# A graph and expert kernel on one core: the first expert slot's first layer, tile by tile

## The chip, the cores and the metric

The kernel runs on one core of a Trainium2 chip. The metric is the device time of one execution in microseconds; lower is better. A core has a matrix engine (PE, with its weight loads shown as PEld), a vector engine (DVE), a scalar engine (ACT), a general engine (POOL) and a queue engine (SP) that here only issues DMAs. Each engine works through its own queue in order. Matmul results go to PSUM, an on-chip memory that PE writes and that DVE and ACT read; everything else is kept in SBUF. Engines are held in step by semaphores: an instruction waits until those that it depends on have ended.

## What is computed

The reference takes 2048 tokens of 256 features and 67584 weighted edges, and does two steps:

```python
x = x + gnn(layernorm(x))      # out[dst] += w * x[src], plus a bias per node
x = x + ffn(layernorm(x))      # 8 experts, the best 2 of a token, mixed by their shares

# ffn, for the experts that a token is sent to:
xe = xn * ln_g + ln_b
h  = gelu(xe @ W1 + b1)        # 256 -> 1024
y  = h @ W2 + b2               # 1024 -> 256
out += share * y
```

The change lies in the second step, in the first expert slot that is worked on.

## The kernel before

**The first half** (to about 230 us) turns the edge list into dense 128x128 blocks and multiplies them with the normalized tokens; dense() (line 375) does the last of these matmuls, and add (line 386) adds them into acc on DVE.

**Routing and slots.** The 2048 tokens are routed in two batches: first_b, the first 10 blocks of 128 tokens, and last_b, the other 6. For each batch DVE takes the two best experts of each token and gives every choice a place in its expert's list. The experts then work in *slots*: a slot is 256 rows (TT = 2 tiles of P = 128) of one expert. Three slots (EARLY = 3) begin before the second batch is routed: whole[0], whole[1] and whole[2], filled from first_b alone. Later slots are loaded by load_slot (line 989), and some at the end hold one tile only (128 rows, "half slots").

**What one slot does.** Each step is a function:
- get_rows (line 978): POOL issues one indirect DMA per tile that gathers the rows of the slot into xs. In the first slots the features come from x1_d, the shares from sh_d.
- turn_rows (line 1006): PE transposes xs, two 128x128 blocks per tile (KD = 2), into the PSUM tile px, after some "warm" matmuls of the identity. scale_rows (line 1023): two DVE instructions of 128x256 scale and shift px into xeT, one for each k.
- layer_1 (line 1044): for each of 8 chunks c (KH = 8), PE multiplies two k-blocks of W1 with xeT into a new PSUM tile ph of 128x256 (a pool of 3 such tiles, ps_h), and ACT applies Gelu with a bias and writes hT[:, c]. A matmul on f32 data shows as two instructions, so a chunk is 4 instructions and a layer 32. A dictionary "between" says what else is to be emitted before a given chunk.
- set_weights (line 1031) prepares each row's share, and layer_2 (line 1059) multiplies hT with W2, tile by tile, scales on DVE (line 1070) and sends the rows out by an indirect DMA (line 1075).

**What sets the order.** From line 697 on the code stands under tc.manual_schedule for all engines but POOL: each of PE, DVE, ACT and SP works through its instructions in the order in which the code emits them. Which instruction waits for which is worked out by the framework from the tiles that they read and write.

**The stage of the change** (lines 1154 to 1195). In order of the code: the last add of the first half; the shares of first_b; POOL's gathers for the three early slots; then

```python
roots(last_b)                      # ACT
turn_rows(whole[0], 6)             # PE: 6 warm matmuls, 4 transposes; DVE: 2 scales
enlist_rows(first_b)               # DVE, f16, 128x2560
count(first_b); take_seen(last_b)  # DVE
...                                # put_acc on SP; scales, logits, best, select of last_b on DVE
hT = layer_1(whole[0], {4: list_batch_0, 7: lambda: sum_counts(last_b)})
```

list_batch_0 (line 1168) emits list_rows(first_b), 20 matmuls of the two lists that enlist_rows and enlist_low made, and an ACT copy of the result. sum_counts (line 779) is PE's counting of last_b and needs sel, the end of DVE's chain of small instructions. After layer_1 come ACT's scale_recs and two table loads, DVE's places and lists of last_b, PE's transposes for whole[1] (head, line 1019), and layer_2 of whole[0].

Of the kernel before, what the change touches and what calls it, by code (L numbers as in the profile page):

```python
# [10 lines left out]
F32 = mybir.dt.float32  # L11
# [3 lines left out]
AF = mybir.ActivationFunctionType  # L15
OP = mybir.AluOpType
# [6 lines left out]
P = 128  # L23
# [4 lines left out]
def kernel(  # L28
# [30 lines left out]
    nc = tc.nc  # L59
# [5 lines left out]
    KD = D // P  # L65
    KH = H // P
# [13 lines left out]
    TS = 256  # L80
# [71 lines left out]
    ident = consts.tile([P, P], F32, name="ident")  # L152
# [239 lines left out]
    with tc.manual_schedule(engines=ALL):  # L392
# [99 lines left out]
        for n in range(NH):  # L492
# [32 lines left out]
            g, k = divmod(n - NB // 2, NB // 2)  # L525
            if g >= 0:
                late.append(dense(GROUPS[g], 2 * k))
            if n == 0:
# [9 lines left out]
                for k in range(KD):  # L538
                    nc.tensor.matmul(tr[:, nt:nt + NE], ones, wr_sb[:, k, :], start=(k == 0),
                                     stop=(k == KD - 1))  # L540
# [4 lines left out]
                for lo, m in ((0, KH), (KH, KD), (KH + KD, KD)):  # L545
# [9 lines left out]
                    op0=OP.mult, op1=OP.add)  # L555
# [42 lines left out]
    with tc.If(n_used < E):  # L598
# [4 lines left out]
        for b in range(NB):  # L603
            nc.vector.tensor_scalar(acc[:, b, :D], acc[:, b, :D], nv_c[:, b:b + 1], None,
                                    op0=OP.add)
# [9 lines left out]
        with tc.tile_pool(name="any", bufs=2) as anyp, tc.tile_pool(  # L615
            name="ps_any", bufs=2, space=PSUM
# [4 lines left out]
            with tc.For_i(0, E // P, 1) as t:  # L621
# [18 lines left out]
                for b in range(NB):  # L640
                    hot = anyp.tile([P, P], F32, name="hot")
                    nc.vector.tensor_scalar(hot, iota_p, s_b[:, b:b + 1], w_t, op0=OP.is_equal,
                                            op1=OP.mult)
# [9 lines left out]
    slotp = right("slot", 2)  # L653
    ps_x = ctx.enter_context(tc.tile_pool(name="ps_x", bufs=1, side="right", space=PSUM))
# [6 lines left out]
    def new_set(pool, i, n=TT):  # L661
        return (
            pool.tile([P, n, RW], F32, name=f"xs{i}"),
            pool.tile([P, KD, H], F32, name=f"w1_{i}"),
            pool.tile([P, KH, D], F32, name=f"w2_{i}"),
            pool.tile([P, KH + 2 * KD], F32, name=f"ec{i}"),
            pool.tile([P, D], F32, name=f"b2_{i}"),
        )
# [14 lines left out]
    sets = [new_set(wpool, i) for i in range(AHEAD + 1)]  # L683
    tos = [wpool.tile([P, TT], I32, name=f"to_i{i}") for i in range(AHEAD + 8)]
    heads = [new_head(wpool, i) for i in range(2)]

    LAST = SURE - EARLY - 2
    whole = []
    for i in range(EARLY + NF):
        k = i - EARLY if i - EARLY < LAST else i - EARLY + 2  # L690
# [6 lines left out]
    with tc.manual_schedule(engines=ALL - {ET.Pool}):  # L697
# [10 lines left out]
        def batch(i, b, n):  # L708
            return {"i": i, "b": b, "n": n, "full": [P, n, NE]}
# [62 lines left out]
        def count(s):  # L772

            sel = s["sel"]
            more = route.tile([P, NE], F32, name=f"more{s['i']}", bufs=1)
            nc.vector.tensor_reduce(more, sel.rearrange("p b e -> p e b"), AX.X, OP.add)
            nc.vector.tensor_add(seen, seen, more)

        def sum_counts(s):

            sel, seen_b = s["sel"], s["seen"]
            s["pc"] = pc = counts[:, s["i"], :s["n"], :]
            nc.tensor.matmul(pc, before, sel, start=True, stop=False)
            nc.tensor.matmul(pc, ones_b, seen_b[:, None, :].to_broadcast(s["full"]), start=False,
                             stop=False)
            for d in range(1, s["n"]):
                nc.tensor.matmul(pc[:, d:, :], ones_b, sel[:, :s["n"] - d, :], start=False,
                                 stop=(d == s["n"] - 1))
            s["all"] = counts[:, 2 + s["i"], 0, :]
            nc.tensor.matmul(s["all"], ones_b, seen_b, start=True, stop=False)  # L790
            for j in range(s["n"]):
                nc.tensor.matmul(s["all"], ones_b, sel[:, j, :], start=False,
                                 stop=(j == s["n"] - 1))
# [74 lines left out]
        def enlist_rows(s):  # L868
            n, in_hi = s["n"] * 2, s["in"][1]
            hot = [P, n, P // 2, 2]  # L870
            tk = tok1[:, s["b"]:s["b"] + s["n"], :].rearrange("p b (i t) -> p (b i) t", t=2)
            nc.vector.tensor_tensor(split(in_hi), split(in_hi), tk[:, :, None, :].to_broadcast(hot),
                                    OP.mult)
# [132 lines left out]
        def turn_rows(s, warm=0):  # L1006


            xs = sets[s.set][0]
            pt = ps_x.tile([P, KD, TS], F32, name="px")  # L1010
            for i in range(warm):
                nc.tensor.matmul(pt[:, 0, :P], ident, ident, start=True, stop=True)
            for t in range(s.n):
                for k in range(KD):
                    nc.tensor.transpose(pt[:, k, t * P:(t + 1) * P],  # L1015
                                        xs[:, t, k * P:(k + 1) * P], ident)
            scale_rows(s, pt)
# [26 lines left out]
        def layer_1(s, between={}):  # L1044
            xs, w1, w2, ec, b2r = sets[s.set]
            xeT = heads[s.head][0]
            hT = slotp.tile([P, KH, TS], F32, name="hT")
            for c in range(KH):
                if c in between:
                    between[c]()  # L1050
                ph = ps_h.tile([P, TS], F32, name="ph")[:, :s.n * P]
                for k in range(KD):
                    nc.tensor.matmul(ph, w1[:, k, c * P:(c + 1) * P], xeT[:, k, :],  # L1053
                                     start=(k == 0), stop=(k == KD - 1))
                nc.scalar.activation(hT[:, c, :s.n * P], ph, AF.Gelu, bias=ec[:, c:c + 1],  # L1055
                                     scale=1.0)
            return hT

        def layer_2(s, hT, put, between={}):
            w2 = sets[s.set][2]  # L1060
            xeT, wt, b2w = heads[s.head]
            for t in range(s.n):
                if t in between:
                    between[t]()
                py = ps_y.tile([P, D], F32, name="py")
                for c in range(KH):
                    nc.tensor.matmul(py, hT[:, c, t * P:(t + 1) * P], w2[:, c, :],  # L1067
                                     start=(c == 0), stop=(c == KH - 1))
                ys = slotp.tile([P, D], F32, name="ys", bufs=4)
                nc.vector.scalar_tensor_tensor(ys, py, wt[:, t:t + 1], b2w[:, t, :], op0=OP.mult,  # L1070
                                               op1=OP.add)
                put(s, t, ys)
# [39 lines left out]
        first_b, last_b = batch(0, 0, NA), batch(1, NA, NB - NA)  # L1112
        warm = route.tile([P, 1], F32, name="warm", bufs=1)
# [15 lines left out]
        for j in range(8, NA):  # L1129
            nc.gpsimd.tensor_scalar(first_b["rec"][:, j, :D], acc[:, j, :D],  # L1130
                                    first_b["r"][:, 1, j:j + 1], first_b["ms"][:, j:j + 1],
                                    op0=OP.mult, op1=OP.add)
# [27 lines left out]
        ps_h = ctx.enter_context(tc.tile_pool(name="ps_h", bufs=3, space=PSUM))  # L1160
        ps_y = ctx.enter_context(tc.tile_pool(name="ps_y", bufs=2, space=PSUM))
        roots(last_b)
        turn_rows(whole[0], 6)
        enlist_rows(first_b)
        count(first_b)
        take_seen(last_b)

# [7 lines left out]
        best(last_b, 0)  # L1175
        best(last_b, 1)
        select(last_b)
        hT = layer_1(whole[0], {4: list_batch_0, 7: lambda: sum_counts(last_b)})
        scale_recs(last_b, range(NB - NA))
        shares(last_b)  # L1180
        nc.scalar.activation(warm, eps_sb, AF.Gelu)
# [12 lines left out]
        hT = layer_1(whole[1], {3: lambda: list_rows(last_b)})  # L1194
# [17 lines left out]
        for u in range(3, SURE - 2):  # L1212
            k = u - (SURE - 2) + len(extra) + 1
            run_slot(whole[u], whole[u + 1], whole[u + 2], *(extra[k:k + 1] if k >= 0 else []),
                     between={4: partial(head, extra[k - 1])} if k > 0 else {})
# [5 lines left out]
    with ExitStack() as nest:  # L1221
        for u in range(SURE - 2, len(whole)):
            s = whole[u]
# [15 lines left out]
    with tc.manual_schedule(engines=ALL - {ET.Pool}):  # L1239
        for q in range(4):  # L1240
            r = slice(q * N // 4, (q + 1) * N // 4)
            nc.sync.dma_start(out[r, :], y_d[r, :])
        for f, y, rows, n in zip(finals, y_rows, (y_d, out), (N + TS, N)):
            get_rows(f, y, rows, n)
            hT = layer_1(f)
# [27 lines left out]
```

## Time and profile before

| | |
|---|---|
| median of 3 timed runs | 496.37 us (496.15 to 496.52) |
| the profiled execution | 494.19 us |
| its span | 492.4 us |
| mean granted clock of PE | 0.979 |
| PE busy | 447.5 us, 91% of the span |
| DVE, ACT, POOL busy | 273.2, 197.5, 164.0 us |
| mean DMA rate | 210 GB/s |

Times in the timeline are counted from the start of the span. "Busy" sums the lengths of an engine's instructions; matmuls overlap, and the length of one includes its drain (an f32 matmul of 256 columns in layer_1 shows 379 ns, while one follows the other in 216). "[1.48 <-DMA xs<-x_d,to_i]" behind a row says that the engine stood idle 1.48 us before this row and that the DMA into xs ended the wait. A number behind "x" counts the instructions that were merged into a row. In names, "hT<-ph,ec" reads "writes hT from ph and ec".

Around the change, PE ends the dense matmuls at 230.0 us, runs the warm matmuls and the transposes of whole[0] until 233.7, layer 1 of whole[0] with list_rows and sum_counts between its chunks from 234.3 to 242.9, the transposes of whole[1] at 242.94, and layer 2 of whole[0] from 243.38.

### The profile page before, as it was taken

To read this page: it belongs to the slowest core of one execution; us is meant where nothing else is said; L and a number is where in the kernel's file an instruction comes from. 1 tells how busy PE (TensorE), PEld (TensorE's weight loads), DVE (VectorE), ACT (ScalarE), POOL (GpSimd) and SP (SyncE) were. 2 spreads that over 40 slices of the span, in tenths; PEclk is the share of its full clock that TensorE was granted. 3 is DMA by queue.
4 is the path that set the end of the run, shared out by engine and by line. 5 is a ranking of instruction groups with operands and counts; after the bars stand their busy time and mean duration, and the time that the engine had idled before them with its cause. 6 is when DMAs were issued, how large, how long until landed. Compare 5 with 4: busy or idle time off the path is not lost. (4 is left out here: it accounts for less than half of the span.)

```text
span 492.4 us, 12148 instructions
## 1 busy us (share of the span) xinstructions
PE 447.5 (91%) x5008; PEld 382.5 (78%) x5008; DVE 273.2 (55%) x563; ACT 197.5 (40%) x480; POOL 164.0 (33%) x133
## 2 busy tenths in 40 slices
PE   1678897889999999998999999999999999999992
PEld 0567785667777888886888888888888888888882
DVE  6899999999999994256762321343332222210011
ACT  2467867563423220066572233333333333333330
POOL 6670733404040000003724433455333344421231
PEclk9986799999999999999999999999999999999998
DMA  3758767776766575995339987999998767721521
GB/s 107 237 162 234 231 201 212 249 235 206 216 201 204 176 220 187 349 339 136 91 118 269 331 237 208 269 358 343 346 352 251 206 166 218 202 51 15 164 74 32
DMA packets 87220, 103.41 MB, mean 210 GB/s; under 512 B 9792, under 2 KB 77488, under 8 KB 85040
## 3 DMA queue, kind: packets, MB, share of 16 engines
q1 hardware_dynamic: 79072, 88.95, 56.5%
q0 software_dynamic: 8048, 13.51, 11.9%
q8 instruction: 44, 0.72, 0.6%
q14 instruction: 24, 0.20, 0.1%
q10 hardware_dynamic: 32, 0.04, 0.0%
HBM read 75.11 MB, written 29.47 MB: 212 GB/s over the span
## 5 line engine op out<-in xcount | busy, mean ns | idle before, releaser
L1053 PE MATMUL ph<-xeT,w 128*128 128x256 f32 (+1 forms) x576 | 122.7, 369 | 3.7 <-PEq L1227 1.3
L1067 PE MATMUL py<-w,hT 128*128 128x256 f32 x544 | 120.4, 379 | 0.0
L1053 PEld LDWEIGHTS ph<-xeT,w 128*128 128x128 f32 x576 | 103.7, 190 | 18.3 <-issue 3.0
L1055 ACT ACTIVATE hT<-ph,ec 128x256 f32<-128x256 f32 (+1 forms) x144 | 65.9, 462 | 129.0 <-PE ph L1053 74.7
L1067 PEld LDWEIGHTS py<-w,hT 128*128 128x128 f32 x544 | 102.1, 190 | 13.2
L1075 POOL DMA_INDIRECT y_d<-ys,to_i x30 | 48.0, 1602 | 114.1 <-DVE ys L1070 76.4
L382 PE MATMUL py<-xn_lo,ac 128*128 128x264 f32 x352 | 84.9, 394 | 0.0
L382 PEld LDWEIGHTS py<-xn_lo,ac 128*128 128x128 f32 x352 | 65.1, 190 | 12.5 <-ACT ar L369 0.2
L327 DVE TENSOR_TENSOR hl<-k,iota_b 128x4096 bf16<-128x4096 bf16 x32 | 73.1, 2283 | 0.0
L366 PE MATMUL pa<-hl,hr 128*32 128x128 bf16 x3072 | 57.5, 236 | 12.8 <-DVE hr L342 10.0
L366 PEld LDWEIGHTS <-hr 128*32 128x32 bf16 x3072 | 50.3, 106 | 23.6 <-DVE hr L342 17.3
L1070 DVE SCALAR_TENSOR_TENSOR ys<-py,wt,b2w 128x256 f32<-128x256 f32 x34 | 16.3, 483 | 79.9 <-PE py L1067 76.6
L342 DVE TENSOR_TENSOR hr<-eq,w 128x3072 bf16<-128x3072 bf16 x32 | 56.3, 1758 | 2.0 <-ACT w L319 0.5
L1027 DVE TENSOR_SCALAR xeT<-px,ec 128x256 f32<-128x256 f32 (+1 forms) x38 | 18.4, 525 | 67.0 <-PE px L1015 67.0
L369 ACT COPY ar<-pa 128x512 f32<-128x512 f32 x64 | 34.9, 585 | 22.9 <-PE pa L366 17.2
L242 POOL DMA_INDIRECT win_s<-in_src,at_i x8 | 13.4, 1676 | 76.7 <-DVE at_i L238 64.6
L980 POOL DMA_INDIRECT xs<-xr_d,to_i x32 | 33.4, 1043 | 15.8 <-DMA xr_d<-rec 6.3
L382 PE MATMUL py<-xn_hi,ac 128*128 128x264 f32 x160 | 36.5, 388 | 0.3 <-PEq L598 0.3
L387 DVE TENSOR_TENSOR acc<-acc,py 128x528 f32<-128x528 f32 x37 | 25.8, 700 | 19.1 <-PE py L382 19.1
L382 PEld LDWEIGHTS py<-xn_hi,ac 128*128 128x128 f32 x160 | 30.2, 190 | 5.7 <-PEq L598 0.7
L1042 ACT ACTIVATE b2w<-b,wt 128x256 f32<-128x256 f32 x36 | 16.3, 500 | 25.7 <-DVE wt L1040 25.7
L334 DVE TENSOR_TENSOR eq<-k,iota_b 128x1024 bf16<-128x1024 bf16 x32 | 21.9, 683 | 0.0
(216 smaller groups left out, 329.4 us busy)
## 6 DMA issues: line engine op xcount, KB each, us to landing
w<-in_L_ffn_W SPq DMA_DIRECT2D x40, 1024.0 KB, 8.9
ad<-ar SPq DMA_DIRECT2D x32, 512.0 KB, 4.1
ac<-ad SPq DMA_DIRECT2D x16, 1024.0 KB, 5.3
b<-in_L_ffn_b SPq DMA_DIRECT2D x20, 128.0 KB, 8.8
acc<-in_x SPq DMA_DIRECT2D x4, 512.0 KB, 6.1
out<-y_d SPq DMA_DIRECT2D x4, 512.0 KB, 7.3
xr_d<-rec SPq DMA_DIRECT2D x1, 1300.0 KB
y_d<-acc SPq DMA_DIRECT2D x1, 1024.0 KB
```

The costliest lines, as they stand in the source:

```text
L327: nc.vector.tensor_tensor(hl.rearrange("p g (n t) -> p g n t", t=2), two(k2[:, 0], g, P), pair(P), OP.is_equal)
L334: nc.vector.tensor_tensor(eq.rearrange("p g (n t) -> p g n t", t=2), two(k2[:, 1], g, RK), pair(RK), OP.is_equal)
L342: nc.vector.tensor_tensor(hr.rearrange("p g i (n t) -> p (g i) n t", t=2), eq[:, :, None, :].to_broadcast([P, GH, 3, RK]), w[:, :, None, : ...
L366: nc.tensor.matmul(pa[j * RK:(j + 1) * RK, m, :], hr[:, g, i, :], hl[:, g, :], start=(i == 0), stop=(i == 2), tile_position=(0, j * RK))
L369: nc.scalar.copy(ar[:, m0:m0 + 4, :], pa)
L382: nc.tensor.matmul(pa[:, i, :DX], acs[c][:, b + i, :], xn(c), start=(c == blocks[0]), stop=(c == blocks[-1]))
L387: nc.vector.tensor_add(acc[:, b:b + 2, :], acc[:, b:b + 2, :], pa[:, :, :DX])
L980: nc.gpsimd.indirect_dma_start(out=(sets[s.set][0] if into is None else into)[:, t, cols], out_offset=None, in_=(xr_d if rows is None else ...
L1053: nc.tensor.matmul(ph, w1[:, k, c * P:(c + 1) * P], xeT[:, k, :], start=(k == 0), stop=(k == KD - 1))
L1055: nc.scalar.activation(hT[:, c, :s.n * P], ph, AF.Gelu, bias=ec[:, c:c + 1], scale=1.0)
L1067: nc.tensor.matmul(py, hT[:, c, t * P:(t + 1) * P], w2[:, c, :], start=(c == 0), stop=(c == KH - 1))
L1075: st = nc.gpsimd.indirect_dma_start(out=y_d[:, :], out_offset=bass.IndirectOffsetOnAxis(ap=tos[s.to][:, t:t + 1], axis=0), in_=ys, in_offs ...
```

## The change

Two new functions take the place of turn_rows and layer_1 for whole[0] only. turn_tile transposes and scales one tile of 128 rows; layer_1_tile runs layer 1 on 128 rows. One px tile and one hT tile are now allocated by the caller. Two chunks share one ph tile of 128x256: an even chunk writes its first 128 columns, the odd one after it the other 128, and each has a Gelu of its own. Tile 0 is turned first, its layer 1 follows; before chunk 4 of tile 0, tile 1 is turned and scaled. On DVE enlist_rows(first_b) comes between the two scalings. Layer 1 of tile 1 stands where layer_1 stood, with list_batch_0 before its chunk 2 (it was 4) and sum_counts(last_b) before its chunk 7, as before.

```diff
+        def turn_tile(s, pt, t, warm=0):
+            xs, w1, w2, ec, b2r = sets[s.set]
+            xeT = heads[s.head][0]
+            rows = slice(t * P, (t + 1) * P)
+            for i in range(warm):
+                nc.tensor.matmul(pt[:, 0, :P], ident, ident, start=True, stop=True)
+            for k in range(KD):
+                nc.tensor.transpose(pt[:, k, rows], xs[:, t, k * P:(k + 1) * P], ident)
+            for k in range(KD):
+                nc.vector.tensor_scalar(xeT[:, k, rows], pt[:, k, rows], ec[:, KH + k:KH + k + 1],
+                                        ec[:, KH + KD + k:KH + KD + k + 1],
+                                        op0=OP.mult, op1=OP.add)
+
+        def layer_1_tile(s, hT, t, between={}):
+            xs, w1, w2, ec, b2r = sets[s.set]
+            xeT = heads[s.head][0]
+            rows = slice(t * P, (t + 1) * P)
+            for c in range(KH):
+                if c in between:
+                    between[c]()
+                if c % 2 == 0:
+                    ph = ps_h.tile([P, TS], F32, name="ph").rearrange("p (i r) -> p i r", r=P)
+                for k in range(KD):
+                    nc.tensor.matmul(ph[:, c % 2, :], w1[:, k, c * P:(c + 1) * P], xeT[:, k, rows],
+                                     start=(k == 0), stop=(k == KD - 1))
+                nc.scalar.activation(hT[:, c, rows], ph[:, c % 2, :], AF.Gelu, bias=ec[:, c:c + 1],
+                                     scale=1.0)
...
-        turn_rows(whole[0], 6)
+        pt = ps_x.tile([P, KD, TS], F32, name="px")
+        hT = slotp.tile([P, KH, TS], F32, name="hT")
+        turn_tile(whole[0], pt, 0, 6)
         enlist_rows(first_b)
+        layer_1_tile(whole[0], hT, 0, {4: lambda: turn_tile(whole[0], pt, 1)})
         count(first_b)
         take_seen(last_b)
...
-        hT = layer_1(whole[0], {4: list_batch_0, 7: lambda: sum_counts(last_b)})
+        layer_1_tile(whole[0], hT, 1, {2: list_batch_0, 7: lambda: sum_counts(last_b)})
```

## The prediction

> **What bounds the kernel now.** I read the page's table of engines first (PE busy 447.5 us of the 492.4 us span, 91%), then the waits of PE from 230 us to the end, then the timeline of PE, DVE and ACT around 230 us. The list of PE's waits in that stretch is short:
>
> ```profile
> PE px L1015 <- DMA xs<-x_d,to_i: 1.5, 1, 1.5
> PE ph L1053 <- PEq L1227: 1.3, 1, 1.3
> PE ph L1053 <- PEq L1221: 1.0, 1, 1.0
> PE ph L1053 <- ACT hT L1055: 0.8, 2, 0.4
> PE ph L1053 <- DVE xeT L1027: 0.6, 1, 0.6
> ```
>
> (Columns: total us, times, longest.) From 234.3 us on PE runs almost without a gap until the tail, and no weight load or gather ever makes it wait. So what moves PE's clock time at 243 us moves the end by as much, as long as loads and DVE move with it; SP's loads mostly wait for PE themselves ("SPq L975 <- PE py L1067", 52.3 us in total), and the first loaded slot has its weights issued by 263.4 us and uses them at 279.5. The two waits of this list that the change touches are the first and the last. PE's timeline has them in place:
>
> ```profile
> 230.02 1.50 PE L1012 MATMUL px<-ident 128*128 128x128 f32 x12
> 231.36 0.38 PE L1015 MATMUL px<-ident,xs 128*128 128x128 f32 x2
> 233.22 0.44 PE L1015 MATMUL px<-ident,xs 128*128 128x128 f32 x2 [1.48 <-DMA xs<-x_d,to_i]
> 234.30 3.74 PE L1053 MATMUL ph<-xeT,w 128*128 128x256 f32 x16 [0.64 <-DVE xeT L1027]
> 237.88 1.28 PE L879 MATMUL listed<-in_hi,in_lo 128*128 128x128 f16 x20
> ```
>
> (Start, length; a length includes the drain of the last matmul.) Rows 0 to 127 are turned at 231.36, rows 128 to 255 only when their gather has landed at 233.22, and layer 1 starts at 234.30. The transposes of the next slot, which end this stage on PE, start at 242.94.
>
> **What the change gives.** After it, layer 1 of tile 0 needs only the first two transposes: they end at 231.74, DVE scales 128x128 in 402 ns (the shortest of the L1027 group, its 128x128 form), and PE starts at about 232.24, 2.06 us earlier. Between chunks 3 and 4 the gather of tile 1 has long landed, so the 1.48 us wait goes.
>
> The price of the narrower matmuls can be read from the kernel's own half slots, which run layer 1 at 128 columns: 447.19 to 450.76 for 32 instructions, 3.57 us, 0.112 us each. Two tiles take 7.14 us. A whole slot takes 6.91 (265.26 to 272.17). So splitting costs PE 0.23 us. ACT issues 16 Gelus of 0.368 us where it had 8 of 0.47; PE needs 0.446 us for a chunk of one tile, so ACT keeps up. DVE runs four 0.40 us scales for two of 0.54, in time in which it waits anyway (2.69 us before 233.70). If nothing else happened, the transposes of the next slot would start at 232.24 + 0.09 (the second half of the first scale) + 7.14 + 0.22 (two transposes) + 1.11 (list_rows, 237.88 to 238.99) + 0.35 (sum_counts) = 241.15 instead of 242.94: **1.79 us gained**.
>
> **What it adds, and what decides.** layer_1_tile puts two chunks into one ph tile: chunk c even into its first half, chunk c odd into its second. In program order that is matmuls of c, Gelu of c, matmuls of c+1, Gelu of c+1, all on the same tile. Is PE allowed to write the second half while ACT reads the first? No operand forbids it. But the trace has one place built like this, pk, into which f's two halves are turned one after the other:
>
> ```profile
> 9.93 0.35 ACT L288 CAST k<-pk 128x256 bf16<-128x256 f32 x1
> 10.06 0.29 DVE L471 TENSOR_TENSOR f<-cl,b_i 128x128 f32<-128x128 f32 x1 [1.21 <-ACT cl L274]
> 10.46 0.18 PEld L287 LDWEIGHTS pk<-ident,f 128*128 128x128 f32 x1 [1.32 <-ACT k L288]
> 10.49 0.45 PE L287 MATMUL pk<-ident,f 128*128 128x128 f32 x1 [1.05 <-DVE f L471]
> ```
>
> The second transpose needs f, which DVE writes; it takes nothing from k, the copy that ACT makes of pk's first part. Yet its weight load is put down to that copy. I read it as a wait of the writer of one part of a PSUM tile for the reader of another part. So I expect every odd chunk to wait for the Gelu of the even chunk before it, and as PE works in order, nothing passes it: the next even chunk, list_rows, the transposes, all stand behind.
>
> The price of that wait, from the half slots and from a place where PE did wait for a Gelu:
>
> ```profile
> 440.08 3.81 PE L1053 MATMUL ph<-xeT,w 128*128 128x128 f32 x32 [0.95 <-PEq L1221]
> 447.19 3.73 PE L1053 MATMUL ph<-xeT,w 128*128 128x128 f32 x32
> ```
> ```profile
> 440.85 3.45 ACT L1055 ACTIVATE hT<-ph,ec 128x128 f32<-128x128 f32 x8 [6.08 <-PE ph L1053]
> 447.88 3.44 ACT L1055 ACTIVATE hT<-ph,ec 128x128 f32<-128x128 f32 x8 [3.58 <-PE ph L1053]
> ```
> ```profile
> 328.81 1.19 ACT L1055 ACTIVATE hT<-ph,ec 128x256 f32<-128x256 f32 x3
> 329.32 1.13 PE L1053 MATMUL ph<-xeT,w 128*128 128x256 f32 x4 [0.40 <-ACT hT L1055]
> ```
>
> A Gelu starts 0.69 us after its chunk's first matmul (447.19 to 447.88), 0.77 after a standstill (440.08 to 440.85), lasts 0.368, and PE goes on 0.04 after its end (328.81 + 0.47 = 329.28, then 329.32). An odd chunk thus starts 0.69 + 0.37 + 0.04 = 1.10 us after the even one, and takes 0.446 + 0.08 for the cold start. **A pair takes 1.62 us instead of 0.89: 0.73 us more, eight times.** The whole stage, step by step, on PE:
> - Pair 0-1 of tile 0 from 232.24. Its first Gelu can't start before ACT's table load of 1.28 us, which starts at 232.65 today and was hidden before; it ends at 233.93. Odd chunk at 234.35, end 234.88.
> - Pair 2-3 to 236.50; turn_tile of tile 1, 0.22, to 236.72; two pairs to 239.97. Its DVE scale takes 0.71 and is ready at 237.7, before 239.97. enlist_rows, 1.48 us on DVE, now runs before that scale, from 232.5 to 234.0, in DVE's idle time.
> - Tile 1: pair 0-1 to 241.60, list_rows 1.11 to 242.71, two pairs to 245.96, chunk 6 to 246.40. sum_counts (0.35) stands before chunk 7 and fills part of its wait; chunk 7 starts at 246.40 - 0.45 + 1.10 = 247.05 and ends at 247.58. DVE has sel, which sum_counts needs, by 237.7 + 4.4 (236.01 to 240.41 today) = 242.1.
>
> The next slot's transposes start at 247.58 instead of 242.94: **4.64 us later**, the 1.79 gained having been spent. DVE's chain, which restarts on sum_counts, moves by 4.8 with it, and so does SP's put_recs and loads; they have slack. No DMA is moved past another: POOL's gathers are issued as before. They run 1.39 and 1.67 us instead of 1.0 where DVE works on f16 beside them, so another of them will be the long one; POOL's queue is empty from 245.4 to 254.0, which hides it.
>
> The unknown is the length of the wait, since no row shows it at this shape. From below: the cold start is hidden, 0.08 less per pair, 0.6 in all. From above: the Gelu takes the 0.47 of the wide form, 0.1 more per pair, 0.8 in all. Below these lies no wait at all, which is the first rival. I take the half-slot rows, which have the very shape.
>
> The profiled execution took 494.19 us (span 492.4 and 1.8 around it); with 4.64 it is 498.83. The median of the timed runs, 496.37, lies 2.18 above the profiled one, so I add 4.64 there: **501.0 us**.
>
> The Trainium skill, "PSUM — Partial Sum Buffer", section "PSUM bank collisions raise a hardware error", speaks against this change: two engines in one 2 KiB bank at once are an error even at different columns, and it advises guarding PSUM by bank, not by address. By that rule a ph tile's halves must take turns, and the sum is 501.0; by address alone it would be 494.6. The pk rows agree with it, by one wait.
>
> **The rivals.** (1) *No wait between the halves*, faster: PE may write one half while ACT reads the other. For it: xeT's two halves are followed separately in this stage (PE starts at 234.30, while DVE's second scale runs to 234.69), and the pk row is one instance, with DVE's f ending at 10.35 right beside it. Against: that is SBUF, and the load there names ACT. Price: 496.37 - 1.79 = 494.6. It decides if an odd chunk follows its even one in 0.45 us.
>
> (2) *The clock falls as well.* The stretch is left with PE working some 55% of its time (0.89 of 1.62 us) for 15 us. The windows of 4 us show what pauses can do:
>
> ```profile
> 24.00:28.00 4.00, 1.69 (x51) 1.51 (x39) 3.92 (x7) 1.80 (x4) 1.68 (x1) 0.97 0.23 31
> 28.00:32.00 4.00, 4.00 (x107) 3.56 (x106) 3.35 (x5) 2.77 (x10) 3.25 (x2) 0.60 0.49 146
> 84.00:88.00 4.00, 2.40 (x80) 1.72 (x81) 3.93 (x10) 0.91 (x3) 0.00 (x0) 1.00 0.64 160
> ```
>
> (Third column PE busy; the clock is the third from the end.) After 2.3 us of idle time it was 0.60; at 2.40 of 4 us busy it stayed 1.00, as it did with 2.14 busy at 232 to 236. Pauses here are 0.65 us, so I expect 1.00. If it halved for four pairs, each would grow by some 1.1 us (8 matmuls of 0.112 doubled, and slower drains), 4.4 in all: about 505.5. The skill's "TensorE: Matmul & The Clock Gate", "A second HAM failure mode: psum-queue depth-cycling", tells of just such short idles between groups making the clock swing; by it the sum would be 505.5, by the nearest row 501.0.
>
> **How the numbers follow.** Forecast 0.82 (501.0, own range 499.8 to 502.4), rival 1 0.06 (494.6), rival 2 0.10 (505.5), and 0.02 for a mixture in which a part of the waits is covered and the time stays. A measurement of this kernel tells about 0.2%, 1 us, from no change. Faster 0.06, same 0.02, slower 0.92. The range covers the forecast with the bounds of the wait, and the nearer part of rival 2: 499.4 to 503.4.
>
> **What would show it.** In the profile after: layer 1's matmuls start at 232.2 and come in pairs 1.6 us apart; PE's waits have a new line, ph from ACT hT, eight times, of some 0.5 us each (1.10 less the 0.61 in which the profile counts an even chunk as busy); the wait for xs is gone; the next slot's transposes start near 247.6. If that line is missing and they start near 241.2, rival 1 holds and the pk row was misread. A clock under 1.00 between 232 and 250 is rival 2.

## The result

The kernel before took 495.7 us (median of 8 runs, 493.45 to 496.59) and the changed kernel 499.7 us (median of 8, 498.56 to 501.67). The ratio is 1.0091 with a 95% interval of 1.0072 to 1.011: the change costs 3.6 to 5.5 us. (A ratio here and below is a measure of its own and not the quotient of the two medians; the two differ by up to 0.2%.)

The profiled execution of the changed kernel took 499.65 us (span 497.8), 5.46 us above the one of before. PE is still the engine that sets the end, with 2.3 us more of busy time:

```profile
PE 449.8 (90%) x5040; PEld 384.8 (77%) x5040; DVE 273.5 (55%) x565; ACT 199.0 (40%) x488; POOL 165.7 (33%) x133
```

PE's waits from 230 us to the end (columns: total us, times, longest):

```profile
PE ph L1086 <- ACT hT L1088: 4.1, 7, 1.3
PE ph L1053 <- PEq L1262: 1.0, 1, 1.0
PE ph L1053 <- PEq L1256: 1.0, 1, 1.0
PE ph L1053 <- ACT hT L1055: 0.8, 2, 0.4
PE ph L1086 <- DVE xeT L1070: 0.5, 1, 0.5
```

The wait for xs, 1.5 us before, is gone. In its place stands a line that was not there: ph waits for hT, that is, matmuls that write a ph tile wait for a Gelu, 4.1 us in all. PE's timeline shows where:

```profile
231.05 0.38 PE L1068 MATMUL px<-ident,xs 128*128 128x128 f32 x2
231.94 0.81 PE L1086 MATMUL ph<-xeT,w 128*128 128x128 f32 x4 [0.50 <-DVE xeT L1070]
234.06 1.79 PE L1086 MATMUL ph<-xeT,w 128*128 128x128 f32 x8 [1.32 <-ACT hT L1088]
236.31 1.22 PE L1086 MATMUL ph<-xeT,w 128*128 128x128 f32 x4 [0.46 <-ACT hT L1088]
...
238.86 1.16 PE L1086 MATMUL ph<-xeT,w 128*128 128x128 f32 x8 [0.46 <-ACT hT L1088]
240.47 1.16 PE L1086 MATMUL ph<-xeT,w 128*128 128x128 f32 x8 [0.46 <-ACT hT L1088]
242.09 0.71 PE L1086 MATMUL ph<-xeT,w 128*128 128x128 f32 x4 [0.46 <-ACT hT L1088]
242.64 1.28 PE L879 MATMUL listed<-in_hi,in_lo 128*128 128x128 f16 x20
...
248.11 0.71 PE L1086 MATMUL ph<-xeT,w 128*128 128x128 f32 x4
248.66 0.60 PE L1015 MATMUL px<-ident,xs 128*128 128x128 f32 x4
```

Each row of x8 is an odd chunk with the even chunk after it, and the stop stands in front of the odd one. Rows 238.86, 240.47 and 242.09 are 1.61 and 1.62 us apart. The next slot's transposes are the measure of the whole stage. They start 17.61 us after the first transposes (231.05 to 248.66); before the change it was 11.58 (231.36 to 242.94). The row that ends the stage in the profile before:

```profile
242.94 0.60 PE L1015 MATMUL px<-ident,xs 128*128 128x128 f32 x4
```

Two rows stand out. Eight matmuls take 1.79 us at 234.06 and 1.16 at 238.86; four take 1.22 at 236.31 and 0.71 at 242.09. The windows of 4 us say why (the third column is PE's busy time, the third from the end the granted clock):

```profile
232.00:236.00 4.00, 2.54 (x12) 2.03 (x12) 1.60 (x2) 2.46 (x6) 3.16 (x3) 0.80 1.17 219
236.00:240.00 4.00, 3.23 (x18) 2.87 (x18) 1.87 (x9) 1.36 (x4) 3.01 (x4) 0.77 0.38 117
240.00:244.00 4.00, 3.09 (x35) 2.87 (x35) 2.63 (x14) 1.51 (x5) 3.09 (x4) 1.00 0.04 2
```

If the granted clock is either whole or half, a mean of 0.80 and of 0.77 makes some 3.4 us at half clock in these two windows, (0.20 + 0.23) x 4 us x 2. Narrower windows bear this out: the clock is 0.91 from 234.0 to 234.5, 0.50 from there to 237.0, 0.59 from 237.0 to 238.0 and 1.00 after it, that is, one stretch at half clock from 234.41 to 237.82. In the profile before, both windows had 1.00.

### The profile page after: what moved, and what is told of

Same layout as the page of the kernel before. It is cut to its first block, busy times and chain, and to the rows that moved or that the text cites. A ratio compares the mean times of both kernels' runs of the same rounds, so it can differ in the third digit from the quotient of the medians.

```text
span 497.8 us, 12221 instructions
## 1 busy us (share of the span) xinstructions
PE 449.8 (90%) x5040; PEld 384.8 (77%) x5040; DVE 273.5 (55%) x565; ACT 199.0 (40%) x488; POOL 165.7 (33%) x133
## 5 line engine op out<-in xcount | busy, mean ns | idle before, releaser
L1053 PE MATMUL ph<-xeT,w 128*128 128x256 f32 (+1 forms) x544 | 115.1, 368 | 2.8 <-PEq L1262 1.0
L1055 ACT ACTIVATE hT<-ph,ec 128x256 f32<-128x256 f32 (+1 forms) x136 | 61.9, 460 | 123.6 <-PE ph L1053 69.7
L1053 PEld LDWEIGHTS ph<-xeT,w 128*128 128x128 f32 x544 | 97.9, 190 | 16.4 <-issue 2.7
L1027 DVE TENSOR_SCALAR xeT<-px,ec 128x256 f32<-128x256 f32 (+1 forms) x36 | 17.4, 525 | 64.4 <-PE px L1015 64.4
```

## The experiments

**Theory.** The framework holds the writer of a PSUM tile until all readers of that *tile* that come earlier in the program have ended, whichever part they read. So each odd chunk waits for the Gelu of its even chunk. **Rivals:** the narrow matmuls and Gelus cost the time by themselves; or the wait goes by smaller parts of PSUM than the tile; or the loss is clock.

The kernels were run in three groups. Each group ran on one chip, another one each time, and each kernel is compared with the kernel before on that same chip. The medians of before were 498.46, 498.63 and 496.16 us in the three groups. The measure in the profiles is the *stage*: from PE's first transposes of whole[0] to those of whole[1].

### First group: whose wait is it

**pair_first**: the tile stays shared, but both chunks are multiplied before either is read.

```diff
-                nc.scalar.activation(hT[:, c, rows], ph[:, c % 2, :], AF.Gelu, bias=ec[:, c:c + 1],
-                                     scale=1.0)
+                if c % 2 == 1:
+                    for i in (0, 1):
+                        nc.scalar.activation(hT[:, c - 1 + i, rows], ph[:, i, :], AF.Gelu,
+                                             bias=ec[:, c - 1 + i:c + i], scale=1.0)
```

> The changed kernel with one thing altered: both chunks of a ph tile are multiplied first, then both Gelus are issued, so that no matmul follows a Gelu on the same ph tile. Theory W (an odd chunk waits for the Gelu of the even chunk in its PSUM tile): the eight waits of PE for hT go, layer 1 of tile 0 starts 2 us earlier than in the kernel before and the next slot's transposes 1.8 us earlier; time 1.8 us under before (ratio about 0.996). Rival N (the pieces themselves are dear: narrower matmuls, 16 Gelus for 8): it stays 4 us over before (ratio 1.008). Rival C (the lower clock between 232 and 240 us makes most of the loss and comes with the early start): the clock is again about 0.8 there, and the time 1 to 2 us over the first figure.

**own_tile**: each chunk has a ph tile of its own, the order is that of the change.

```diff
-                if c % 2 == 0:
-                    ph = ps_h.tile([P, TS], F32, name="ph").rearrange("p (i r) -> p i r", r=P)
+                ph = ps_h.tile([P, TS], F32, name="ph")[:, :P]
...
```

(The matmuls write this ph and the Gelu reads it.)

> The changed kernel, but every chunk has a ph tile of its own (the pool has 3), matmuls and Gelus in the same order as in the changed kernel. Theory W: no waits between neighbours; only chunk 3 of tile 0 waits, for the first Gelu, which stands behind ACT's table load: about 0.7 us once. The next slot's transposes 1.0 us earlier than before; time 1.0 us under before (ratio 0.998). Rival N: 4 us over before, since widths and counts are the same as in the changed kernel.

**wait_only**: the kernel before, 256 rows at once, with the sharing alone added: two chunks in one ph tile of 2 x 256 columns, in the order of the change. As the tiles of a pool have one size, the later slots' ph tiles become 2 x 256 too, of which they use the first half. layer_1_paired is layer_1 with these lines:

```diff
+                if c % 2 == 0:
+                    ph = ps_h.tile([P, 2, TS], F32, name="ph")
+                for k in range(KD):
+                    nc.tensor.matmul(ph[:, c % 2, :], w1[:, k, c * P:(c + 1) * P], xeT[:, k, :],
+                                     start=(k == 0), stop=(k == KD - 1))
...
-        hT = layer_1(whole[0], {4: list_batch_0, 7: lambda: sum_counts(last_b)})
+        hT = layer_1_paired(whole[0], {4: list_batch_0, 7: lambda: sum_counts(last_b)})
```

> The kernel before with the sharing alone: layer 1 of the first slot stays 256 columns wide and whole, but two chunks share one ph tile of 2x256, Gelu of the even one emitted before the matmuls of the odd one. Theory W: an even chunk's Gelu starts 1.12 us after its first matmul and takes 0.47, so a pair takes 2.60 us for 1.73, four times; sum_counts covers 0.35 of the last: 3.1 us over before (ratio 1.006), with four waits of PE for hT of about 0.6 us. Rival N: no change, as no piece is narrower.

**three_banks**: the change with one ph tile of three parts, 2 KiB apart; chunk c writes part c mod 3, so that neighbours in time never share a part. ph3 is a single tile of 128 x 3 x 512 f32.

```diff
-                if c % 2 == 0:
-                    ph = ps_h.tile([P, TS], F32, name="ph").rearrange("p (i r) -> p i r", r=P)
+                ph = ph3[:, c % 3, :P]
...
```

> The changed kernel, but all chunks of the first slot write one single PSUM tile of 3x512 f32, chunk c its part c mod 3. It asks what the wait goes by. If it goes by the tile as a whole, every chunk waits for the Gelu before it: 16 pauses of 0.65 us, some 9 us over before. If it goes by 2 KiB parts of the tile (512 f32 in each partition), neighbours don't meet, and it is as with a tile for each chunk: 1.0 us under before. Rival N: 4 us over before.

Measured:

| kernel | median us (range, runs) | ratio to before (95%) | stage us | mean granted clock in it | waits of PE for a Gelu in the stage, us |
|---|---|---|---|---|---|
| pair_first | 503.25 (500.55 to 505.14, 8) | 1.0081 (1.0052 to 1.011) | 16.26 | 0.91 | none |
| own_tile | 504.19 (503.07 to 506.08, 6) | 1.0113 (1.0082 to 1.0144) | 19.16 | 0.83 | 0.42 for the first Gelu, 0.15; then late ones, below |
| wait_only | 504.96 (504.06 to 506.41, 6) | 1.0118 (1.009 to 1.0147) | 20.29 | 0.83 | at the odd chunks: 0.56, 0.56, 3.47, 0.23 |
| three_banks | 511.17 (508.1 to 513.48, 6) | 1.0243 (1.0205 to 1.028) | 26.29 | 0.67 | 1.31 once, 0.46 eleven times |

The waits answer the question. First pair_first, PE's timeline:

```profile
236.27 2.15 PE L1086 MATMUL ph<-xeT,w 128*128 128x128 f32 x16 [0.50 <-DVE xeT L1070]
238.25 0.38 PE L1068 MATMUL px<-ident,xs 128*128 128x128 f32 x2
238.47 2.84 PE L1086 MATMUL ph<-xeT,w 128*128 128x128 f32 x24
241.15 1.28 PE L879 MATMUL listed<-in_hi,in_lo 128*128 128x128 f16 x20
```

Same split, same shared tiles, another order of emission: 16 and 24 matmuls run without a stop, the 24 in 2.68 us (238.47 to 241.15), 0.112 us each. The narrow matmuls are not the cost. Now three_banks, its line in the list of PE's waits:

```profile
PE ph L1085 <- ACT hT L1087: 5.4, 10, 1.3
```

No two neighbouring chunks share a 2 KiB part here, yet every chunk after the first stops unless other work of PE stands in front of it: twelve of fifteen, ten by this line and two that the timeline puts to "issue" with the same 0.46 us. In own_tile, where the three parts are three tiles, neighbours do not wait. The wait goes by the tile, not by a part of it.

The times did not follow, though. pair_first and own_tile have lost these waits and are as slow as the change, where ratios of 0.996 and 0.998 were expected; wait_only and three_banks lost more than the 3.1 and 9 us expected, with the clock at half for a third or two thirds of the stage. In pair_first and own_tile the cause is another one, and neither theory had it. ACT's timeline of pair_first, the copy of the lists:

```profile
249.22 0.27 ACT L1207 COPY lists<-listed 128x128 f32<-128x128 f32 x1 [6.64 <-remote]
```

list_rows, which it copies, starts at 241.15 on PE and the next matmuls follow at 242.27. In the profile before, this copy comes 0.2 us after that point (PE 238.99, ACT 239.19):

```profile
239.19 0.27 ACT L1170 COPY lists<-listed 128x128 f32<-128x128 f32 x1 [0.64 <-PE listed L879]
```

In pair_first it comes 6.95 us after it. ACT has nothing in front of it in its queue, and "remote" says that the profile finds no instruction whose end released it. Later Gelus stand behind the copy, sum_counts and the last matmuls come in pieces with gaps that the profile puts to "issue", and the stage takes 16.26 us. In own_tile the same copy is late, and PE then waits for the Gelu behind it:

```profile
248.54 2.07 PE L1085 MATMUL ph<-xeT,w 128*128 128x128 f32 x8 [5.25 <-ACT hT L1087]
```

(Its stop of 0.78 before that, put to "issue", is such a wait too: the Gelu of the chunk that had this tile before starts at 242.16, after ACT has stood idle for 1.13 us, and ends 0.05 us before PE goes on.) wait_only has the late copy as well (at 249.09, after an idle time of 4.30 us). I read this as an end signal of PE that reached ACT some microseconds late in these three. The profile's ends of matmuls are modelled, so the record of list_rows alone would allow that its work ended late; but in own_tile PE has stood idle since 243.29 when the copy starts at 247.95.

### Second group: is it the change or the chip

The kernels before and after were repeated unchanged as **before_again** and **after_again**, pair_first as **pair_again**. **split_only** turns both tiles first, as before, then runs layer 1 tile by tile with both chunks ahead of their Gelus, as in pair_first: the split without the early start and without the wait.

Against pair_first:

```diff
         turn_tile(whole[0], pt, 0, 6)
+        turn_tile(whole[0], pt, 1)
         enlist_rows(first_b)
-        layer_1_tile(whole[0], hT, 0, {4: lambda: turn_tile(whole[0], pt, 1)})
+        layer_1_tile(whole[0], hT, 0)
```

> The kernel before once more, unchanged, for a profile and times on the same chip as the next three. In pair_first, own_tile and wait_only ACT's copy of the lists began 3.7 to 7.5 us after PE's last matmul of list_rows, though nothing else is in its way; in before and after it began 0.03 us after. Theory P (the late copy is a property of the place or the chip of that call): it shows here too, by 3 us or more, in every kernel of this call or in none. Theory Q (it is made by the altered order of PE's work): it is absent here and in after_again, and present in pair_again. Time: ratio 1.000.

> The changed kernel once more, unchanged. Seven or eight waits of PE for hT, 0.46 us each, as in its first profile; the time 4.5 us over before (ratio 1.009). Whether the clock falls to 0.5 for a window of 3.4 us near 234 us again, as in its first profile, is open: with it the next slot's transposes start 6 us later than in before, without it 4.6. By theory Q the copy of the lists follows PE within 0.1 us; by theory P it is late as in the others.

> The kernel of pair_first once more. Its waits between the halves were gone in its profile and its PE reached list_rows 1.7 us sooner after the first transposes than the kernel before, and then the copy of the lists came 6.8 us late. Theory Q: late again by some 6 us, ratio 1.008. Theory P: if before_again shows no late copy, neither does this, and the time is 1.8 us under before (ratio 0.996).

> The changed kernel as in pair_first (two chunks, then two Gelus, no wait between the halves), but both tiles are turned before layer 1 begins, as in the kernel before. It leaves the price of the split alone: 64 matmul instructions of 128 columns for 32 of 256, 0.23 us by the half slots, ratio 1.0005. By theory Q the copy of the lists is late by 4 to 7 us here too, since the same dense run of narrow matmuls stands before list_rows, and the ratio is 1.01; by theory P it is as before_again.

Measured:

| kernel | median us (range, runs) | ratio to before (95%) | stage us | copy starts after PE went on from the lists, us |
|---|---|---|---|---|
| before_again | 498.17 (496.97 to 500.41, 12) | 1.0 (0.9978 to 1.0022) | 13.02 | 2.62 |
| after_again | 505.29 (503.07 to 509.91, 6) | 1.0141 (1.0111 to 1.017) | 23.48 | 0.25 |
| pair_again | 501.74 (500.08 to 502.79, 6) | 1.0076 (1.0051 to 1.0101) | 16.37 | 8.38 |
| split_only | 501.78 (497.92 to 503.85, 12) | 1.0063 (1.0038 to 1.0088) | 13.41 | 2.89 |

The kernel before shows the late copy on this chip as well; in its first profile it did not. ACT and PE of before_again:

```profile
243.21 0.27 ACT L1170 COPY lists<-listed 128x128 f32<-128x128 f32 x1 [3.06 <-PE ph L1053]
244.64 0.84 ACT L1055 ACTIVATE hT<-ph,ec 128x256 f32<-128x256 f32 x2 [1.17 <-PE counts L792]
```
```profile
239.47 1.28 PE L879 MATMUL listed<-in_hi,in_lo 128*128 128x128 f16 x20
240.59 2.81 PE L1053 MATMUL ph<-xeT,w 128*128 128x256 f32 x12
...
245.16 1.13 PE L1053 MATMUL ph<-xeT,w 128*128 128x256 f32 x4 [1.43 <-issue]
```

The copy comes 2.62 us after PE has gone on from the lists (240.59), and PE itself stands for 1.43 us in front of chunk 7. The profile puts that to "issue", but the rows explain it: chunk 7 takes the ph tile of chunk 4 (there are three), and the Gelu of chunk 4, the first of ACT's row at 244.64, ends some 0.05 us before PE goes on. In pair_first and pair_again PE also stops in the midst of a chunk and of the counting, and there no row explains it. So the late signal is not made by the change. But it takes different sums from the kernels: 1.44 us of the stage from before (13.02 against 11.58 in its first profile), and more from pair_again, which reached list_rows earlier in the stage and whose copy then came the later (238.24 to 246.62).

split_only was to tell the price of the split alone. Its stage is 0.39 us longer than that of before_again, but this is a sum of several things: it waited 0.56 us longer for the second gather (1.88 and 1.32), began layer 1 0.25 us after the second transposes where before_again needed 1.07, and lost somewhat more in gaps at the end. PE's own pace says it better: 60 narrow instructions in 6.76 us are 7.21 us for 64, and 28 wide ones in 6.23 us are 7.12 for 32, so the split itself costs PE some 0.1 us. Layer 2 behind it takes 8.02 us for the same 32 matmuls where before_again has 7.07; the clock there is 0.71 in the window 248 to 252. Stage and layer 2 make 1.3 us, and the two profiled executions lie 1.45 apart (499.86 and 498.41); what the ratio's 1.9 to 4.4 us hold beyond that isn't placed.

What lies beside the late signals? In all these profiles POOL runs its six gathers of the shares at that time, one each 1.3 us, and the last of the late signals come in 1.2 to 1.7 us after the last gather has ended: in before_again it ends at 246.41 and DVE learns of PE's counting at 247.62, in split_only 247.30 and 248.51 (DVE), in pair_first 249.22 and 250.95 (DVE again), in own_tile 246.57 and 247.95 (the copy), in wait_only 247.79 and 249.09 (the copy). three_banks and after_again, on the same two chips, come to list_rows only when the gathers are at their end (247.94 after 245.57, and 247.60 with the last one ending at 247.77), and their copies start 0.25 us after PE has gone on. Yet not every signal beside the gathers is late: three_banks' Gelus of that time start 1.26 us after their chunk (240.21 and 241.47, 241.89 and 243.15), just as at the same clock after the gathers (255.29 and 256.55). POOL's last row of pair_again, which ends at 245.18, and ACT's copy, 1.44 us after it:

```profile
244.19 0.99 POOL L980 DMA_INDIRECT xs<-sh_d,to_i  x1 [0.30 <-issue]
```
```profile
246.62 0.27 ACT L1207 COPY lists<-listed 128x128 f32<-128x128 f32 x1 [7.99 <-remote]
```

That made a new theory: the signals are late *because of* these gathers. Against it stood the first profiles of before and after, which have the same gathers and no late signal.

after_again shows the third cost at its largest. Its windows:

```profile
244.00:248.00 4.00, 1.95 (x13) 1.69 (x13) 0.79 (x5) 0.89 (x3) 2.98 (x3) 0.74 0.04 2
248.00:252.00 4.00, 3.54 (x26) 3.25 (x24) 0.00 (x0) 0.84 (x3) 0.00 (x0) 0.50 0.02 1
252.00:256.00 4.00, 3.54 (x21) 3.19 (x21) 0.00 (x0) 1.10 (x3) 0.00 (x0) 0.50 0.00 0
```

The clock is at 0.50 for two whole windows, and the stage is 5.9 us longer than the first profile of the same program showed (23.48 against 17.61); 1.6 us of that is one pause of 2.05 where 0.46 was usual. That pause is a late signal again, and it came in before the last gather had ended (247.77):

```profile
246.17 0.37 ACT L1088 ACTIVATE hT<-ph,ec 128x128 f32<-128x128 f32 x1 [1.68 <-remote]
```

The mean clock of the whole stage is 0.68, some 15 us of it at half; in the first profile it was 0.90.

### Third group: without the gathers of the shares

Three kernels leave out the six gathers of the shares (the first three slots then have no shares, so their part of the output is missing): **before_noshare**, **after_noshare** and **pair_noshare** (pair_first without them). **pair_two** is pair_first with the first slot's two gathers only.

```diff
-        for u in range(EARLY):
-            get_rows(whole[u], rows=sh_d, n=NA * P, cols=slice(D, RW))
```

> The kernel before without POOL's six gathers of the shares in this stage (the first three slots then lack their shares, so a part of the computation is left out). Theory G (PE's end signals come late because of these gathers, and arrive some 1.3 us after the last of them): ACT's copy of the lists starts within 0.3 us of list_rows' end, the next slot's transposes come 11.6 us after the first ones, and if the kernel before itself shows the late signal on this chip (13.0 us as in before_again), this run is 1 to 2.5 us faster, 0.3 to 0.5% (ratio 0.995 to 0.998). Rival (the lateness belongs to the chip or to the place in the program, not to the gathers): the copy starts 2 to 3 us after list_rows again, and the time is within 0.2% of before.

> The changed kernel without POOL's six gathers of the shares in this stage (the first three slots lack their shares). Both theories keep the pauses of 0.46 us at each odd chunk, since these come from the shared ph tile. G: no late copy of the lists; transposes 17 to 18 us after the first ones with one clock window at half, 16.2 with none; 4.6 to 6.5 us above before_noshare (ratio to before 1.005 to 1.01). Rival: a late signal of 1.5 us or more shows in at least one place of the stage, 7 us or more above before_noshare (ratio 1.012 to 1.016).

> The version in which both chunks of a ph tile are multiplied before either is read (no pause for a Gelu), without POOL's six gathers of the shares (the first three slots lack their shares). G: the copy of the lists is on time, the next transposes come 9.5 to 10.5 us after the first ones, and the time is 1.0 to 1.8 us under before_noshare: the 1.79 us that the prediction worked out for the early start are seen at last (ratio to before 0.990 to 0.996). Rival: the copy comes 6 to 8 us after list_rows again, transposes near 16.3 us, ratio 1.007 to 1.009.

> The same version (both chunks of a tile before their Gelus) with two of the six gathers, those of the first slot (the second and third slot lack their shares). G, by size: the stall ends 1.2 to 1.5 us after the second gather, some 4 to 5 us sooner than with six, so that the copy of the lists is late by 2 to 4 us at most or not at all, the next transposes come 10 to 13 us after the first ones, ratio 0.993 to 1.001. Rival: as with all six, copy late by 6 to 8 us, transposes near 16.3 us, ratio 1.007 to 1.009.

Measured:

| kernel | median us (range, runs) | ratio to before (95%) | stage us |
|---|---|---|---|
| before_noshare | 494.98 (494.37 to 498.16, 12) | 0.9999 (0.9978 to 1.0021) | 12.27 |
| after_noshare | 501.51 (498.96 to 502.0, 6) | 1.0111 (1.0078 to 1.0144) | 16.25 |
| pair_noshare | 492.76 (491.79 to 493.57, 10) | 0.9938 (0.9917 to 0.9959) | 10.05 |
| pair_two | 492.79 (491.61 to 493.76, 12) | 0.9943 (0.9922 to 0.9965) | 10.05 |

No copy is late in any of the four. pair_noshare on PE:

```profile
231.84 0.38 PE L1068 MATMUL px<-ident,xs 128*128 128x128 f32 x2
232.72 2.15 PE L1086 MATMUL ph<-xeT,w 128*128 128x128 f32 x16 [0.50 <-DVE xeT L1070]
...
234.93 2.84 PE L1086 MATMUL ph<-xeT,w 128*128 128x128 f32 x24
237.61 1.28 PE L879 MATMUL listed<-in_hi,in_lo 128*128 128x128 f16 x20
238.72 2.45 PE L1086 MATMUL ph<-xeT,w 128*128 128x128 f32 x20
...
241.89 0.60 PE L1015 MATMUL px<-ident,xs 128*128 128x128 f32 x4
```

It runs through the stage without a stop, in 10.05 us, 1.53 less than the first profile of before and 2.22 less than before_noshare, whose wait for xs was longer this time (2.17 us). The medians of these two differ by 2.22 us as well. So the early start is worth its time when neither the shared tile nor a late signal takes it back. after_noshare:

```profile
233.75 0.81 PE L1086 MATMUL ph<-xeT,w 128*128 128x128 f32 x4 [0.50 <-DVE xeT L1070]
235.88 1.16 PE L1086 MATMUL ph<-xeT,w 128*128 128x128 f32 x8 [1.31 <-ACT hT L1088]
...
248.57 0.71 PE L1086 MATMUL ph<-xeT,w 128*128 128x128 f32 x4
249.12 0.60 PE L1015 MATMUL px<-ident,xs 128*128 128x128 f32 x4
```

The pauses are all there (list of waits: 4.1 us, 7 times, as in the change), the clock is 1.00 in every window from 228 to 264 us, and the stage is 16.25 us. Between pair_noshare and this kernel only the order of the Gelus differs: 8.75 us of median, 6.20 of stage.

The medians hold more than the stages: after_noshare lies 6.53 us above before_noshare, its profiled execution (499.94 us) 4.99 above that one's (494.95).

What this group does *not* settle is the late signal. The rival (late again without the gathers) failed in all four, and most of the numbers that the theory gave were met; off were the ratio of after_noshare, 1.0111 where 1.005 to 1.01 was expected, the stage of before_noshare, 12.27 for 11.6 (its longer wait for xs), and the lead of pair_noshare over before_noshare, 2.22 us for 1.0 to 1.8. Yet a third reading fits as well: that this chip, like the one of the first profiles, shows no late signals with any number of gathers. Two results speak for it. In pair_two two of the gathers run just when the copy is due:

```profile
237.61 1.00 POOL L980 DMA_INDIRECT xs<-sh_d,to_i  x1 [0.30 <-DMA y_d<-acc]
238.92 1.00 POOL L980 DMA_INDIRECT xs<-sh_d,to_i  x1 [0.30 <-issue]
```
```profile
238.37 0.27 ACT L1206 COPY lists<-listed 128x128 f32<-128x128 f32 x1 [0.49 <-PE listed L879]
```

The copy came in the middle of them, 0.2 us after PE had gone on (238.17). And before_noshare is no faster than before on its chip to within 1 us (0.9978 to 1.0021), so six gathers cost before little or nothing there. pair_first with all its gathers was not run on this chip. Whether it is faster there than before is open; on the two chips on which it was measured it is slower, 1.0081 and 1.0076, and a version that computes everything and beats the kernel before has not been shown.

## Why the prediction was right, step by step

The forecast was 501.0 us, 4.64 over before. Measured: 499.7, by the ratio 3.6 to 5.5 us over before. The direction, the mechanism and nearly every term held; one term was missing from the likeliest sum. That the number came so close is partly luck: the profiled stage grew by 6.03 us and not by 4.64, and the same change cost 7.0 us on the chip of the second group.

- **The early start.** Predicted: layer 1 begins 0.88 us after the first transposes (232.24 and 231.36) and the wait for xs goes. Measured: 0.89, and it is gone. The gain was not to be seen in the changed kernel; pair_noshare's stage, 10.05 us, is near the 9.79 that the sum without waits gave (241.15 less 231.36).
- **The wait by tile.** Predicted from one pk row, which was thin: f, which that transpose needs in any case, ended at 10.35, after the copy (10.28), so f alone would have held it as long. Measured: stops at every odd chunk of the change; none when both chunks are emitted ahead of the Gelus (pair_first) or, but for two short stops while the three tiles were all in use, when each has its own tile (own_tile); present when only the sharing is added (wait_only); present across parts 2 KiB apart (three_banks). That shows the wait. The Trainium skill, "PSUM — Partial Sum Buffer", section "PSUM bank collisions raise a hardware error", asks for a guard by bank and quadrant; the wait found here is coarser than that, since three_banks stops too.
- **Its size.** Predicted: 1.62 us per pair, stops of some 0.5. Measured: 1.61 and 1.62, stops of 0.46.
- **The first pair and the table load.** Predicted: odd chunk 2.11 us after layer 1's start, because the first Gelu waits for the table. Measured: 2.12, a stop of 1.32.
- **sum_counts hides part of the last wait.** Predicted: chunk 7 starts 1.10 us after chunk 6. In the trace the row of 246.49 holds chunks 5 and 6, the counting fills the gap, and chunk 7 follows at 248.11 without a stop; the list has seven waits and not eight for this reason.
- **DVE, POOL.** The second scale started at 238.00 and sel at 242.76, both somewhat later than predicted (done by 237.7, there by 242.1) but long before the counting at 247.49. A gather grew to 2.08 us beside DVE's f16 instruction, as "another of them" was to. None of this reached PE.
- **The sum.** Predicted stage 16.22 us (247.58 less 231.36). after_noshare, at full clock: 16.25. The change: 17.61.

**The missing term is the clock.** "Pauses here are 0.65 us, so I expect 1.00", and the whole fall was given 4.4 us and one chance in ten. The profiled execution had 3.4 us at half clock, which with 17.61 - 16.22 cost 1.39 us (1.36 against after_noshare); after_again had some 15 us and lost 5.7 by the same sum (23.48 less 16.22 and less 1.6 of a late signal). Both are some 0.4 us for each us at half clock. So the second rival was not an alternative but an addition of varying size. What the timed runs hold of it can't be read: their medians lie 4.0 us apart, the two profiles 5.46. The row that was used against it, 84 to 88 us, had a single window's busy share; the share does not decide. The section "A second HAM failure mode: psum-queue depth-cycling" of the skill's "TensorE: Matmul & The Clock Gate" speaks of short idles between groups that make the clock swing. The profiles of the change agree, 0.80 and 0.77; after_noshare, with the same pauses and 1.00, does not.

**Not foreseen at all** was the late signal. It changes no sign here, but on the chip of the second group it moved the ratio to 1.0141 (1.0111 to 1.017), 7.0 us on 498.63, together with the clock, which had the larger part. That is just the upper edge of the stated range (503.4 is 7.0 above 496.37).

## What to carry to other kernels

When two results share one PSUM tile, look at the order of emission: writer, reader, writer makes the second write wait for the first read, whichever parts they touch; writer, writer, reader, reader showed no stop. Split a step at a transfer only if the halves keep their own tiles or that order (here even that was seen to be faster only with gathers of the shares left out), and price a pause between matmuls with its clock: here a pair grew from 0.89 to 1.62 us, and clock cost 1.4 us on top in one profile and some 5.7 in another. When a fix removes the wait that the profile names and the time stays, look at the next consumer's idle time before the theory is dropped.

## What the runs showed of the hardware that was not expected

- **PE's end signals seem to reach other engines late at times.** With the same program, the copy of the lists started 0.2 us after PE had gone on in one profile (before) and 2.62 in another (before_again); in pair_again it was 8.38. In pair_first and pair_again PE had gaps in the same stretch that no wait explains. It was seen in before_again, split_only, pair_first, pair_again, own_tile and wait_only, in each beside POOL's six gathers and ending 1.2 to 1.7 us after the last, and once, 1.6 us late, in after_again before their end; not in three_banks, nor in the four kernels of the third group, nor in the first profiles, whose copies came on time in the midst of the gathers. Whether the gathers, the chip, the kernel's own pace or several of these make it is open.
- **The granted clock's fall is not set by the busy share of a window.** It stayed 1.00 with PE busy 1.19 of 4 us (before_noshare, 232 to 236 us) and with 3.08 of 4 in three windows of after_noshare, and was 0.80 with 2.54 of 4 in the change. It was 0.50 for two windows with 3.54 of 4 busy in after_again, where the matmuls themselves, being slower, fill the time. The same stops of 0.46 us and one of 1.3 gave three outcomes: no fall in after_noshare, 3.4 us at half in the change, some 15 us in after_again. What decides between them was not found.
